# Two graph attention layers: the vectors W1 a1 and W1 a2 by dots on VectorE, a fourth tile of adj, weight work in single steps, constants made later

## The chip, the cores and the metric

The kernel runs on one core of a Trainium2 chip. Five engines work beside each other, each on its own list of instructions: TensorE (PE; its weight loads are counted as PEld), VectorE (DVE), ScalarE (ACT), GpSimd (POOL) and SyncE (SP), which only issues transfers. Transfers (DMAs) are issued by SP, ACT or POOL. The metric is the device time of one launch in microseconds (us); three runs of the kernel before gave 1781.02 us as their median.

## What is computed

```python
f = x @ Wf + bf;  g = x @ Wg + bg
e = jax.nn.relu(f @ g.T)                       # layer 0
attention = softmax(where(adj > 0, e, NEG), axis=1)
x = layernorm(x + attention @ (x @ W + bW))

h = x @ W1                                     # layer 1
e = leaky_relu(h @ a1 + (h @ a2).T, 0.2)
attention = softmax(where(adj > 0, e, NEG), axis=1)
x = layernorm(x + relu(attention @ h))
```

There are 2708 nodes with 1024 features; adj is 2708 x 2708 (int32), symmetric, with about 0.6% of its entries set. All is float32.

## The kernel before

**Algebra.** The score f g^T is x (Wf Wg^T) x^T with bias terms. So a prelude makes M = Wf Wg^T once, the bias rows c3 and rb, and for layer 1 the vectors u1 = W1 a1 and u2 = W1 a2, each repeated on all 128 partitions (`u1b`, `u2b`). Since adj is sparse, the prelude also turns each of its rows into a list of at most 40 neighbours; both layers then gather only these rows of x.

**Prelude, lists.** adj is cut into 22 blocks of 128 rows; the last has 20. For each block, `lists(b)` does: a load by SP into a tile of the pool `adjp` (three buffers), Relu to float on ACT with a row count (`tot`), a product with the falling ramp `iota` on POOL (line 409; block 0's in two cuts), 20 times the eight largest of 136 columns on VectorE (line 412), then the 40 largest of those 160 (five maxima at line 416 with a replacement between them at line 418), and counts (lines 420 and 424). `keep_lists(b - 3)` has ACT turn the list into indices and send it to memory (`LD`).

**Prelude, weights.** `weights()` is a generator whose steps are interleaved with the blocks, one step after each block from block 1 on. `turned` transposes a loaded 128-row tile of a weight matrix by eight TensorE transposes and two ACT copies; the tiles come through the pool `stage` (three buffers), loaded by ACT in the order Wg, Wf, W1. `m_product` is a sixteenth of M (eight products of 128x512), its ACT copy is kept in `late` and done at the next `flush()`. `c_product` makes the bias vectors of one half; its `take` ends with `row_parts`, which splits a row in three bfloat16 parts by casts, subtractions and small DMAs on POOL. bW goes through `row_parts` too. After c_product(0) stands a small product for the scalar `s0` (the ACT copy of tile `s`). Last come W1's eight transposed tiles and `u_product(0)` and `(1)`, whose `take` copies into `u1b` and `u2b`. These go on after the loop where the steps outlast the blocks.

**Order.** The engines' objects `pe`, `dve`, `act`, `pool` and `sp` are wrapped by `InOrder` (line 71 of the page is its helper): what they issue stays in program order on that engine. Instructions issued through `nc.gpsimd` and `nc.vector` are placed by a scheduler. Waits between engines follow from the tiles; a buffer of a pool is written again only when its last reader is done. At the head of POOL's list stand the constants (`ramp`, `stack`, `rep`, `early`, `lower`, `qcol`) and `iota`.

**After the lists.** Lines 454 to 501 rank the nodes by list length (VectorE with five small TensorE products) and write the orders `ids` and `idq`.

**Start of layer 0.** POOL gathers x of block 1 and 0 (`load_x`) and their lists (`load_lists`); VectorE makes `q_dot(1)` and `q_dot(0)`, then a minimum on the lists (`SL0`, in `first_gathers`) which releases the first gathers of neighbours into `ring`. TensorE makes the products with M of block 1 (`two_products`), ACT copies them four times over partitions (`Fr`), and VectorE's `dots` of unit 0 take them. Then follow `f_small` (block 0, in quarters summed by a second product), `x_turn(2)`, `f_product(2)`, the load of W into `Wt`, and a loop over the units: dots on VectorE, exp on ACT, sums over neighbours on TensorE (`po<-ring,st`), products with W (`pm<-Wt,xT`). The page's rows of some 700 matmuls are this loop in both layers. The end of this start reads:

```python
        q_dot(2)
        f_small()
        x_turn(2)
        load_x(3)
        load_lists(4)
        f_product(2)
        spread2 = q_spread(2)
        next(spread2)
        act.dma_start(Wt, W.rearrange("(k p) d -> p k d", p=P))
        dots(units[0], 0, len(units[0].tiles))
```

Of the kernel before, what the change touches and what calls it, by code (L numbers as in the profile page):

```python
# [106 lines left out]
def listed_path(ctx, tc, x, adj, Wf, bf, Wg, bg, W, bW, W1, a1, a2, out):  # L107
# [43 lines left out]
    nc.gpsimd.memset(ones3, 1.0)  # L151
# [4 lines left out]
    nc.gpsimd.memset(quad, 0.0)  # L156
    for q in range(Q):
        rows = slice(32 * q, 32 * q + 32)
        nc.gpsimd.tensor_copy(stack[rows], ident[rows, rows])
        nc.gpsimd.memset(quad[rows, q:q + 1], 1.0)  # L160
    for q in range(Q):
        nc.gpsimd.tensor_copy(rep[:, q, :], stack)
# [4 lines left out]
    nc.gpsimd.memset(ids[:, 0:1], 0)  # L167
# [4 lines left out]
    nc.gpsimd.memset(f1, 0.0)  # L172
# [4 lines left out]
    for t in scores:  # L177
        nc.gpsimd.memset(t, 0.0)
# [15 lines left out]
    with tc.tile_pool(name="pre", bufs=1) as pre:  # L194
        iota = pre.tile([P, N], F32, name="iota")
        nc.gpsimd.iota(iota, pattern=[[-1, N]], base=NONE, channel_multiplier=0,
# [3 lines left out]
        tot = pre.tile([P, NB], F32, name="tot")  # L200
        cnt = pre.tile([P, NB], F32, name="cnt")
# [7 lines left out]
        def ramp(name, count, step, base, dtype=F32, part=0):  # L209
            t = pre.tile([P, count], dtype, name=name)  # L210
            nc.gpsimd.iota(t, pattern=[[step, count]], base=base, channel_multiplier=part,
                           allow_small_or_imprecise_dtypes=True)
            return t

        fours = ramp("fours", QT, 4, 0)
        classes = ramp("classes", NCL, 1, 0)
        lows = ramp("lows", 32, 1, 0)
        highs = pre.tile([P, NG], F32, name="highs")
        rows512 = ramp("rows512", NB, 512, 0)
        part4 = ramp("part4", 1, 0, 0, part=4)  # L220
        lower = pre.tile([P, P], BF16, name="lower")
        nc.gpsimd.memset(lower, 1.0)
        nc.gpsimd.affine_select(lower, lower, pattern=[[1, P]], compare_op=ALU.is_gt, fill=0.0,
                                base=0, channel_multiplier=-1)
        early = pre.tile([P, NB, NB], F32, name="early")
        nc.gpsimd.memset(early, 1.0)
        nc.gpsimd.affine_select(early, early, pattern=[[1, NB], [-1, NB]], compare_op=ALU.is_gt, fill=0.0,
                                base=0, channel_multiplier=0)
        onesb = pre.tile([P, P], BF16, name="onesb")
        nc.gpsimd.memset(onesb, 1.0)  # L230
        qcol = pre.tile([P, 1], F32, name="qcol")
        for q in range(Q):
            nc.gpsimd.memset(qcol[32 * q:32 * q + 32], float(q))

        def fill_highs():
            nc.gpsimd.memset(highs[:, 0:1], float(GROUPS[0]))
            h = highs[:, 1:].rearrange("p (b k) -> p b k", k=4)
            at = 0
            for n, a, b in BLOCKS:
                for k, (g0, g1) in ((0, a), (2, b)):  # L240
                    if g1 == g0 + 1:
                        nc.gpsimd.iota(h[:, at:at + n, k:k + 2], pattern=[[2, n], [1, 2]], base=g0,
                                       channel_multiplier=0, allow_small_or_imprecise_dtypes=True)
                    else:
                        for i, g in enumerate((g0, g1)):
                            nc.gpsimd.memset(h[:, at:at + 1, k + i:k + i + 1], float(g))
                at += n

        with tc.tile_pool(name="adjp", bufs=3) as adjp, tc.tile_pool(name="cands", bufs=2) as cands, \
# [19 lines left out]
            order += [(W1, k) for k in range(KC)]  # L269
# [21 lines left out]

            def weights():


                late = []

                def flush():
                    while late:
                        late.pop(0)()
# [27 lines left out]
                def u_product(h, wT):  # L327

                    half = slice(h * 512, (h + 1) * 512)
                    pm = ps_m.tile([P, H, 512], F32, name="pm")  # L330
                    for i in range(KC):
                        for j in range(2):
                            pe.matmul(pm[64 * j:64 * j + 64, 0, :], ac[:, j, i:i + 1].to_broadcast([P, 64]),
                                      wT[:, i, :], start=(i == 0), stop=(i == KC - 1))

                    def take():
                        for j, u in enumerate((u1b, u2b)):
                            mine, other = 64 * j, 64 - 64 * j
                            act.copy(u[mine:mine + 64, half], pm[mine:mine + 64, 0, :])
                            for q in (0, 32):  # L340
                                act.copy(u[other + q:other + q + 32, half], pm[mine + q:mine + q + 32, 0, :])
                    late.append(take)


                four = pre.tile([32, P], F32, name="four")
                for i, v in enumerate((bg, bf, a1, a2)):
                    act.dma_start(four[8 * i:8 * i + 8], v.rearrange("(k p) -> k p" if i < 2 else "(k p) o -> k (p o)", p=P))
                cols = pre.tile([P, 4, KC], F32, name="cols")
                bgc, bfc, ac = cols[:, 0, :], cols[:, 1, :], cols[:, 2:4, :]
                WgT = {0: half_tile()}  # L350
                for k in range(4):
                    turned(WgT[0][:, :, k * P:(k + 1) * P])
                pt = ps_t.tile([P, 4, P], F32, name="pt")
                pe.transpose(pt[:, 0, :32], four, ident[:32, :32])
                act.copy(cols.rearrange("p v k -> p (v k)"), pt[:, 0, :32])
                yield
                WgT[1] = half_tile()
                for k in range(KC):
                    flush()
                    turned(WfT[:, :, k * P:(k + 1) * P])  # L360
                    if k >= 4:
                        turned(WgT[1][:, :, (k - 4) * P:(k - 3) * P])
                    m_product(k, 0)
                    if k in (2, 5):
                        half = slice(k // 3 * 512, k // 3 * 512 + 512)
                        brow = pre.tile([1, 512], F32, name="rest", bufs=3)
                        act.dma_start(brow, bW[half].rearrange("(o d) -> o d", o=1))
                        row_parts(brow, b3[:, half])
                    yield
                flush()  # L370
# [4 lines left out]
                nc.vector.scalar_tensor_tensor(t, bfc, 1.0, bgc, op0=ALU.mult, op1=ALU.mult, accum_out=t1)  # L375
                pt = ps_t.tile([P, 4, P], F32, name="pt")
                pe.matmul(pt[:, 0, 0:1], ones.to_broadcast([P, P]), t1, start=True, stop=True)
                act.copy(s0, pt[:, 0, 0:1])
                yield
                W1T = None  # L380
                for k in range(KC):
                    flush()
                    if k >= 4:
                        W1T = W1T or half_tile()
                        turned(W1T[:, :, (k - 4) * P:(k - 3) * P])
                    m_product(k, 1)
                    yield
                flush()
                c_product(1)
                yield  # L390
                flush()
                u_product(0, W1T)
                W1T = half_tile()
                for k in range(4):
                    turned(W1T[:, :, k * P:(k + 1) * P])
                yield
                flush()
                u_product(1, W1T)
                yield
                flush()  # L400

            def lists(b):
                n = nsize[b]
                t = adjp.tile([P, N], I32, name="adj")
                sp.dma_start(t[:n], adj[b * P:b * P + n, :])
                k = t.bitcast(F32)
                act.activation(k[:n], t[:n], AF.Relu, accum_out=tot[:n, b:b + 1])
                for cut in ([slice(0, 10 * SEG), slice(10 * SEG, N)] if b == 0 else [slice(0, N)]):
                    nc.gpsimd.tensor_tensor(k[:n, cut], k[:n, cut], iota[:n, cut], op=ALU.mult)  # L409
                cand = cands.tile([P, NSEG, 8], F32, name="cand")  # L410
                for s in range(NSEG):
                    nc.vector.max(cand[:n, s, :], k[:n, s * SEG:min((s + 1) * SEG, N)])  # L412
# [21 lines left out]
            steps = weights()  # L434
            for b in range(NB):
                lists(b)
                if b > 2:
                    keep_lists(b - 3)
                if b == 4:
                    fill_highs()  # L440

                if b > 0:
                    next(steps, None)
            for b in range(NB - 3, NB):
                keep_lists(b)
            for _ in steps:
                pass

        bc = lambda t, k, shape: t.unsqueeze(k).to_broadcast(shape)
        eq = pre.tile([P, NB, NCL], F32, name="eq")
        gt = pre.tile([P, NB, NCL], F32, name="gt")
# [1021 lines left out]
```

## Time and profile before

| what | time |
|---|---|
| median of three runs | 1781.02 us (1780.73 to 1785.28) |
| profiled execution | 1778.93 us |
| its span in the profile | 1777.1 us |
| end of the last list (VectorE) | 205.99 us |
| end of the ids | 217.92 us |
| first sums of unit 0 (TensorE) | 280.58 us |
| first product with W | 293.91 us |

The groups of instructions from 0 to 206 us with each shape by itself (line, engine, operation, tiles, shapes, count, then busy us, mean ns of one, and the idle time before them with what ended it):

```profile
L409 POOL TENSOR_TENSOR adj<-adj,iota 128x2708 f32<-128x2708 f32 x20 | 118.6, 5935 | 22.8 <-ACT adj L71 22.7
L412 DVE MAX8 cand<-adj 128x8 f32<-128x136 f32 x399 | 89.3, 286 | 37.2 <-POOL adj L409 37.2
L71 ACT ACTIVATE adj<-adj 128x2708 f32<-128x2708 int32 x21 | 51.8, 2465 | 25.6 <-DMA adj<-in_adj_dram 25.6
L416 DVE MAX8 L<-cand 128x8 f32<-128x160 f32 x105 | 33.8, 322 | 2.5
L418 DVE MATCH_REPLACE8 cand<-L,cand 128x160 f32<-128x160 f32 x84 | 25.9, 309 | 0.0
```

A mean of one can hold a wait inside a run of instructions: 20 maxima in a row take 4.11 us where nothing else of VectorE's stands between them. Idle time before a group is listed where it ends; it costs only if that engine is late for the end. Of an engine's idle time, the name behind the arrow is the instruction or transfer that came last.

### The profile page before, as it was taken

To read this page: it belongs to the slowest core of one execution; us is meant where nothing else is said; L and a number is where in the kernel's file an instruction comes from. 1 tells how busy PE (TensorE), PEld (TensorE's weight loads), DVE (VectorE), ACT (ScalarE), POOL (GpSimd) and SP (SyncE) were. 2 spreads that over 40 slices of the span, in tenths; PEclk is the share of its full clock that TensorE was granted. 3 is DMA by queue.
4 is the path that set the end of the run, shared out by engine and by line. 5 is a ranking of instruction groups with operands and counts; after the bars stand their busy time and mean duration, and the time that the engine had idled before them with its cause. 6 is when DMAs were issued, how large, how long until landed. Compare 5 with 4: busy or idle time off the path is not lost. (4 is left out here: it accounts for less than half of the span.)

```text
span 1777.1 us, 22911 instructions
## 1 busy us (share of the span) xinstructions
PE 1573.1 (89%) x7313; PEld 667.6 (38%) x7313; DVE 1171.4 (66%) x3539; ACT 636.4 (36%) x861; POOL 1182.5 (67%) x1191
## 2 busy tenths in 40 slices
PE   4999479899999999999999999637989988989996
PEld 2444234344444444444444444213333333333342
DVE  5879855888888888988888887513342433424442
ACT  4544454444444455555555544101111111111111
POOL 7878476467666666666666663177777777777740
PEclk9999779999999999999999999959989999999998
DMA  7646168568777777777777777299999999999960
GB/s 283 237 169 238 40 233 301 208 224 296 282 285 274 264 250 255 280 284 287 279 291 283 268 281 281 103 358 346 363 386 392 392 364 394 384 392 388 366 259 37
DMA packets 149982, 501.86 MB, mean 282 GB/s; under 512 B 32565, under 2 KB 32597, under 8 KB 147144
## 3 DMA queue, kind: packets, MB, share of 16 engines
q0 software_dynamic: 132032, 427.36, 64.8%
q1 hardware_dynamic: 10202, 55.72, 8.3%
q10 hardware_dynamic: 7618, 17.23, 2.7%
q8 instruction: 59, 0.97, 0.2%
q14 instruction: 71, 0.58, 0.1%
HBM read 509.64 MB, written 33.75 MB: 306 GB/s over the span
## 5 line engine op out<-in xcount | busy, mean ns | idle before, releaser
L71 POOL DMA_INDIRECT ring<-in_x_dram,SL x405 | 432.0, 1067 | 256.2 <-issue 89.0
L71 DVE SCALAR_TENSOR_TENSOR j<-ring,Fr 128x1024 bf16<-128x1024 f32 x402 | 494.9, 1231 | 77.0 <-DMA ring<-in_x_dram,SL 49.8
L71 ACT COPY Fr<-pm 32x1024 f32<-32x1024 f32 (+2 forms) x353 | 340.5, 965 | 20.0 <-PE pm L71 15.3
L71 PE MATMUL po<-ring,st 128*32 128x512 f32 x2660 | 338.6, 614 | 0.1
L71 POOL DMA_INDIRECT ring<-T,SL x260 | 259.6, 998 | 83.8 <-issue 58.0
L71 PE MATMUL pm<-M,xT 128*128 128x512 f32 (+1 forms) x704 | 309.7, 617 | 0.4 <-ACT xT L71 0.4
L71 PE MATMUL pm<-Wt,xT 128*128 128x512 f32 (+1 forms) x704 | 303.5, 599 | 0.0
L71 PE MATMUL pm<-M,yT 128*128 128x512 f32 (+1 forms) x704 | 298.5, 595 | 0.3 <-ACT yT L71 0.3
L71 ACT ACTIVATE scores<-scores 128x24 f32<-128x24 f32 (+5 forms) x44 | 9.8, 222 | 640.7 <-DVE scores L71 640.7
L71 PEld LDWEIGHTS pm<-M,yT 128*128 128x128 f32 (+1 forms) x704 | 127.2, 186 | 170.2 <-issue 169.7
L71 PEld LDWEIGHTS pm<-M,xT 128*128 128x128 f32 (+1 forms) x704 | 127.0, 190 | 170.6 <-issue 169.9
L71 PEld LDWEIGHTS pm<-Wt,xT 128*128 128x128 f32 (+1 forms) x704 | 125.0, 186 | 151.8 <-issue 151.4
L71 POOL DMA_INDIRECT more<-T,SL x145 | 144.1, 994 | 44.0 <-issue 32.8
L71 PEld LDWEIGHTS po<-ring,st 128*32 128x32 f32 x2660 | 102.5, 114 | 183.9 <-issue 180.0
L71 DVE TENSOR_SCALAR scores<-ring,f1q 128x2 f32<-128x2 f32 (+5 forms) x98 | 21.8, 245 | 211.3 <-DMA ring<-T,SL 209.6
L409 POOL TENSOR_TENSOR adj<-adj,iota 128x2708 f32<-128x2708 f32 (+3 forms) x23 | 130.5, 5684 | 24.9 <-ACT adj L71 24.8
L71 ACT ACTIVATE y<-po,ri 128x512 f32<-128x512 f32 (+1 forms) x88 | 55.8, 683 | 232.5 <-PE po L71 214.6
L412 DVE MAX8 cand<-adj 128x8 f32<-128x136 f32 (+2 forms) x440 | 97.2, 284 | 37.4 <-POOL adj L409 37.4
L71 PE MATMUL pm<-halfT,WfT 128*128 128x512 f32 x256 | 113.9, 600 | 1.1 <-ACT WfT L71 1.1
L71 POOL DMA_INDIRECT SL<-LD,idq x85 | 85.5, 1006 | 25.8 <-issue 20.9
L71 PE MATMUL pt<-rs,stack 128*32 128x1 f32 x680 | 14.1, 179 | 98.0 <-DVE rs L71 53.4
L71 PE MATMUL po<-more,st 128*32 128x512 f32 x580 | 94.2, 651 | 0.0
(198 smaller groups left out, 1416.9 us busy)
## 6 DMA issues: line engine op xcount, KB each, us to landing
adj<-in_adj_dram SPq DMA_DIRECT2D x21, 1354.0 KB, 5.8
X1S<-z SPq DMA_DIRECT2D x20, 512.0 KB, 6.4
ring<-in_x_dram,SL POOLq DMA_INDIRECT x405, 6.2
u1b<-X1S SPq DMA_DIRECT2D x11, 512.0 KB
rb<-X1S SPq DMA_DIRECT2D x10, 512.0 KB, 7.3
ring<-T,SL POOLq DMA_INDIRECT x260, 7.3
rows<-in_L_gnn_Wg_dram ACTq DMA_DIRECT2D x8, 512.0 KB, 4.5
rows<-in_L_gnn_Wf_dram ACTq DMA_DIRECT2D x8, 512.0 KB, 3.6
```

Source lines behind the costliest of these rows:

```text
L71: made = self.tc.keep_in_program_order(op(*args, **kwargs))
L409: nc.gpsimd.tensor_tensor(k[:n, cut], k[:n, cut], iota[:n, cut], op=ALU.mult)
L412: nc.vector.max(cand[:n, s, :], k[:n, s * SEG:min((s + 1) * SEG, N)])
```

## The change

1. W1 a1 and W1 a2: the eight tiles of W1 and the two u products leave the prelude. W1 is loaded whole by SP into `Wt`, which lies where the weights' pool lay; a1 and a2 are spread over the partitions by two POOL DMAs; 16 dots on VectorE (`u_dots`, 4 of them ahead of `q_dot(1)`, 12 between the two q spreads) make `ucols`, 16 TensorE products with the identity turn them (`u_spread`), four ACT copies write `u1b` and `u2b`. W is loaded into the same `Wt` later, as before, behind these.
2. `adjp` has four buffers. Block 0 is loaded and passed through Relu in two cuts, the products of blocks 0 and 1 are in two cuts; a small Relu before the first load brings ACT's table in.
3. The block of 20 rows lies on 4 x 32 partitions with 677 columns each (five maxima in place of 20, four POOL products, four POOL loads) and is taken as the twelfth of the 22.
4. The steps of `weights()` are single tiles (cost 1) and single products (cost 6); after block i they go on until their sum reaches 2i, from the third block on 6.5i - 13.5. bW is loaded once, ahead.
5. Constants are made behind the first products (at blocks 2 to 5, `highs` at 8), in POOL's program order.
6. Ranking: `same` is first on VectorE, its product with `early` is on POOL. Its tiles lie in a pool of their own.
7. Start of layer 0: block 2 is transposed before the small product, whose first part uses a tile of `ps_s`; `f_product(2)` stands ahead of the small product's second part. The copy `Fr[0, 0]` and the load of W stand after the first u copies.

```diff
-            order += [(W1, k) for k in range(KC)]
...
-        with tc.tile_pool(name="adjp", bufs=3) as adjp, tc.tile_pool(name="cands", bufs=2) as cands, \
+        with tc.tile_pool(name="adjp", bufs=4) as adjp, tc.tile_pool(name="cands", bufs=2) as cands, \
...
+                brow = u1b[0:1, :]
+                act.dma_start(brow, bW.rearrange("(o d) -> o d", o=1))
...
+                if b == NB - 1:
+                    k = tail.bitcast(F32)
+                    act.activation(k, tail, AF.Relu, accum_out=tails)
...
+                    for c in range(4):
+                        rows = slice(32 * c, 32 * c + 32)
+                        pool.tensor_tensor(k[rows], k[rows], iota[rows, c * quarter:(c + 1) * quarter],
+                                                op=ALU.mult)
+                    for s in range(NSEG // 4):
+                        nc.vector.max(cand4[:, s, :], k[:, s * SEG:min((s + 1) * SEG, quarter)])
...
+            act.activation(tot2, ones, AF.Relu)
+            for i, b in enumerate(blocks):
                 lists(b)
...
+                if 2 <= i < 6:
+                    next(some, None)
+                if i == 6:
+                    pool.memset(tail, 0)
+                    for c in range(4):
+                        pool.dma_start(tail[32 * c:32 * c + few, :], adj[N - few:, c * quarter:(c + 1) * quarter])
...
+                if i in (13, 15):
+                    u, a = (u1b, a1) if i == 13 else (u2b, a2)
+                    pool.dma_start(u, a.rearrange("d o -> (d o)").partition_broadcast(P))
+
+                flush()
+                while done < (2 * i if i < 3 else 6.5 * i - 13.5):
+                    cost = next(steps, None)
...
         Wt = new_pool("w0", 1).tile([P, KC, D], F32, name="Wt")
+
+        sp.dma_start(Wt, W1.rearrange("(k p) d -> p k d", p=P))
...
+        ucols = small.tile([P, 2, KC], F32, name="ucols", bufs=1)
+
+        def u_dots(k0, k1):
+            for k in range(k0, k1):
+                for i, u in enumerate((u1b, u2b)):
+                    dot(Wt[:, k, :], u, P, ucols[:, i, k:k + 1])
...
+        u_dots(0, 2)
         q_dot(1)
         q_dot(0)
...
+        for _ in spread1:
+            pass
+        u_dots(2, KC)
+        for _ in spread0:
+            pass
+        xTs[2] = tp.tile([P, KC, P], F32, name="xT")
+        turn2 = turn(xb[2], nrows[2], xTs[2])
+        next(turn2)
+
+
+        small_f = split_product(xTs.pop(0), M, yp.tile([P, D], F32, name="y"), 0,
+                                ps_s.tile([P, H, 512], F32, name="po"))
+        next(small_f)
...
+        next(small_f)
         q_dot(2)
-        f_small()
-        x_turn(2)
         load_x(3)
         load_lists(4)
+        spreads = [u_spread(0), u_spread(1)]
+        next(spreads[0])
         f_product(2)
+        for _ in spreads[0]:
+            pass
+        next(spreads[1])
+        Fr[0, 0] = zs[:, :D]
+        act.copy(Fr[0, 0], flat(whole(small_f)))
+        for _ in spreads[1]:
+            pass
         spread2 = q_spread(2)
         next(spread2)
         act.dma_start(Wt, W.rearrange("(k p) d -> p k d", p=P))
```

## The prediction

> **What bounds the kernel now.** I read the page first, then a table of stages, then waits and timeline of the first 300 us, where the edits lie. From the page:
>
> ```profile
> span 1777.1 us, 22911 instructions
> ...
> PE 1573.1 (89%) x7313; PEld 667.6 (38%) x7313; DVE 1171.4 (66%) x3539; ACT 636.4 (36%) x861; POOL 1182.5 (67%) x1191
> ...
> PE   4999479899999999999999999637989988989996
> PEld 2444234344444444444444444213333333333342
> DVE  5879855888888888988888887513342433424442
> ```
>
> A slice is 44.4 us. The prelude is the first five; from the seventh on TensorE is full. The table of stages (columns: window, length, busy time of each engine, granted clock, DMA share, GB/s) gives the contrast:
>
> ```profile
> 180.00:206.00 26.00, 14.41 (x78) 6.32 (x74) 24.61 (x126) 13.86 (x24) 16.92 (x10) 0.91 0.17 48
> 206.00:230.00 24.00, 8.98 (x48) 6.31 (x49) 12.91 (x36) 6.05 (x11) 8.11 (x8) 0.50 0.11 29
> 380.00:1150.00 770.00, 741.64 (x3260) 314.45 (x3256) 662.47 (x1496) 370.86 (x449) 486.69 (x460) 1.00 0.74 268
> ```
>
> In the steady stage TensorE works 741.64 of 770 us, and nothing there is edited: a microsecond won before it should reach the end, since nothing in it hangs on an absolute time. At the end of the prelude VectorE is the late engine (24.61 of 26), and TensorE's last product of W1 ends at 196.08, 11.4 us before its next work. The 23 us of TensorE work that the change removes are therefore no gain by themselves. What sets the end of the prelude is the chain load of adj, Relu (ACT), product with iota (POOL), maxima (VectorE), block after block. Its waits, from 0 to 206 us (total, times, longest):
>
> ```profile
> DVE cand L412 <- POOL adj L409: 37.4, 13, 12.8
> ...
> POOL adj L409 <- ACT adj L71: 24.8, 11, 7.2
> ...
> ACT s L71 <- PE pt L71: 6.7, 1, 6.7
> ...
> POOL part L256 <- DMA rest<-in_L_gnn_bW_dram: 5.5, 2, 3.5
> ```
>
> Of 206 us VectorE is busy 162.0; 37.4 of the 44 idle are these 13 waits. Where they and the next ones lie, by the timeline (start, length):
>
> ```profile
> 6.76 1.28 ACT L71 ACT_TABLE_LOAD   x1 [6.76 <-DMA adj<-in_adj_dram]
> ...
> 13.85 2.11 DVE L412 MAX8 cand<-adj 128x8 f32<-128x136 f32 x10 [12.77 <-POOL adj L409]
> ...
> 198.02 4.10 DVE L412 MAX8 cand<-adj 20x8 f32<-20x136 f32 x20 [0.28 <-POOL adj L409]
> ...
> 223.47 1.23 DVE L71 SCALAR_TENSOR_TENSOR j<-xb,rb 128x1024 bf16<-128x1024 f32 x1 [5.55 <-DMA xb<-in_x_dram,ids]
> ...
> 244.87 0.22 DVE L71 TENSOR_SCALAR q<-pt,s 128x4 f32<-128x4 f32 x1 [14.64 <-PE pt L71]
> ```
>
> The reader sees a late start, a block of only 20 rows that costs VectorE as much as a full one and comes last, and two holes (5.55 and 14.64) after it.
>
> **What the Trainium skill says.** "ScalarE: Activation LUTs", What ACT_TABLE_LOAD costs, gives about 1283 ns; the trace has 1.28 us, on the path. "DMA: Bandwidth & Descriptors", Latency and other measured facts, gives a transfer a fixed cost of about 2 us; no half load is in this trace to test it. The same page, Issuing engines are not separate DMA queues, says that transfers started by any engine share the 16 DMA engines and interleave: the 4096 KB of W, issued at 264.89 beside gathers, landed near 280.6, 15.7 us, and the DMA view has 412 to 423 GB/s over the stretch. "GPSIMD Engine Reference", Key points, says that GpSimd shares SBUF interfaces with VectorE for instructions of two SBUF inputs; the dots here take 1.21 to 1.23 us with POOL quiet and 1.25 to 1.29 beside gathers, so I price the new dots at 1.27.
>
> **The change, part by part**, on the profiled execution.
>
> *Start.* 1354 KB landed 5.95 us after issue (0.81 to 6.76). With 2 us fixed, half takes an estimated 4.0 and lands at 4.8. Half a Relu is 1.25 (2.46 for all), half a product 3.06 (the row of 128x1360), 0.3 for hand-overs: first maximum at 9.4 instead of 13.85, the table being loaded during the transfer. -4.4. Bounds -2 (halves land together at 6.8) to -5.5.
>
> *Block 1 in halves.* VectorE waited 3.79 at 22.74 for a whole product of 5.94. With half of it, about 1 is left: -2.8.
>
> *Tail of 20 rows.* At the end it takes 198.02 to 205.99, 8.0. In the new layout five maxima (some 1.3), four copies of 0.2 and the same selection (202.16 to 205.99, 3.8) are 5.9: -2.1. Its four products on 677 columns are 5.93/4 each, so POOL gains nothing. Its place in the middle only moves it.
>
> *bW once, early.* POOL's cast waited 3.5 for bW at 53, and the product queued behind made VectorE wait 3.60 at 62.02: -3.5. The second wait (2.0 at 80) hit nothing.
>
> *ACT held behind TensorE.* The copy of s waited 6.74 for TensorE's c product, with the Relu of the next block behind it; POOL then waited 7.22 and VectorE 2.91, 5.40 and 1.69, 10.0 in all. Smaller weight steps and a fourth adj buffer let a Relu through earlier, but the in-order queue and TensorE's pace stay: 6.5 units a block at 145/124 = 1.17 us (the windows up to 206 sum to 168 us of TensorE work; less 8 transposed tiles at 1.15 and two products at 7.03, 23) is 7.6 us a block, as long as VectorE's. I take two thirds, -6.5; bounds 0 and -10.
>
> *Onto POOL.* The constants (5 us between 4.08 and 8.2 plus qcol, hidden behind the first load before) and six DMA issues (four for the tail, two broadcasts; an indirect one takes 1.0) now stand between products: 10 us more in a queue whose mults and row parts take 154. POOL idled about 33 us between 10.76 and 198, so most is absorbed: +2.5, bounds 0 and +10.
>
> End of lists: -4.4 - 2.8 - 2.1 - 3.5 - 6.5 + 2.5 = -16.8, at about 189 instead of 206. The rank work after it, 11.9 us, stays: one product of 0.64 moves to POOL under other work, -0.3.
>
> *W1.* Its load waits for TensorE's last c product. That is paced into the last block's turn, and I place its end at 172 to 182 (TensorE from about 12, 145 busy, 15 to 25 idle; before it idled 12 from 15.9 to 196). With 12 to 15.7 us for 4096 KB it lands at 184 to 198. ids end at about 201, so it's in time. Four dots (5.1) fit into the hole of 5.55, twelve (15.2) into that of 14.64: +0.6. Behind them on VectorE stand q_dot and the minimum that releases the first ring gathers; this is the cover to watch. TensorE gets 16 transposing matmuls of some 0.13 (eight transposes take 1.04), 2 us, in its hole of 9.19 or after.
>
> *Start of layer 0.* f_product of block 2 begins near 255 instead of 264.8 (it needn't wait for the small product's repetition). But the sums of unit 0, at 280.58 before, need exp on ACT, which now stands behind the y copy and four u copies and the z copy (9 x 0.6 = 5 us more): I get 277.5, -2.6. Against it, W is issued behind those copies, near 275.8 instead of 264.9, and lands near 291.5 to 298; its first product is due at 291. TensorE waits 0 to 7; I take 2.6, so this part is 0 (bounds -4 and +5).
>
> Sum: -16.8 - 0.3 + 0.6 + 0 = -16.5. The span 1777.1 becomes 1760.6; the profiled run was 1778.93 and becomes 1762.4. The median of the runs, 1781.02, stands 2.1 above the profiled run: 1764.5, said as 1764.
>
> **Rivals.**
> A. The lists are bound by POOL or by ACT behind TensorE after all: the 6.5 isn't won, the 10 us on POOL cost 5. Then -4.4 - 2.8 - 2.1 - 3.5 + 5 + 0.3 = -7.5: 1773. For it: TensorE's 7.6 and VectorE's 7.5 us a block; POOL's 24.8 us of waits for Relu. Against it: those waits are tied to single places.
> B. Also the start of layer 0 is won, W landing before it is due (at 412 GB/s 4096 KB are 10 us, an end at 286): -16.5 - 4 = 1760; with the whole 10 of the ACT wait 1757. Against it: gathers share the engines.
> C. W1 lands late. The place is VectorE's first four dots: every microsecond after ids + 0.4 delays q_dot, the minimum, each ring gather and all that follows, one for one. It decides from a landing at 201.4; the gain is gone at 218 and at 225 the kernel takes 1788. For that TensorE's last c product must end near 210, which takes over 50 us of idle time in the prelude. If W lands late too (7 instead of 2.6), 206 is enough. For it: TensorE is now paced, not run ahead, and ACT's queue couples it to the blocks. Against it: it idled 12 us before.
> D. The gain is swallowed by a slack before the steady stage. The gathers and TensorE start from ids, and TensorE is full from 380; I see no slack of 10 us. About 1781.
>
> **How the numbers follow.** The forecast has 0.50, A 0.17, B 0.14, C 0.11, D 0.08. 0.3% is 5.3 us, about what a measurement tells from no change: 1775.7 to 1786.4. Faster: the forecast, B and most of A, 0.79. Same: D and a part of A and C, 0.10. Slower: C, 0.11. The likeliest case's own range is 1757 to 1770; holding 8 in 10 with A and B it is 1753 to 1777.
>
> **What would show it.** Right: first maximum at 9 to 10; last selection of a list at 186 to 192; no W1 transposes; W1 landed before ids; no hole over 1 us around the first dots; sums of unit 0 some 17 to 20 us earlier, the same length from there to the end. Wrong: VectorE idle by more than 16 us on adj after its first maximum (A); a wait of VectorE for W1 (C); TensorE waiting over 5 us for W (start of layer 0).

## The result, and the profile after

The changed kernel takes 1781.76 us, the kernel before 1782.62 (medians of 20 runs each); the ratio is 0.9994, with a 95% interval of 0.9982 to 1.0006. No change can be measured, where 1764 was forecast. The profiled execution has a span of 1779.0 us and took 1781.02. For two of the experiments below, e8 and e9, every kernel was about 13% slower on their chip (the kernel before: 2014.87 us) and the profiled executions were slow ones, so of these two only the ratio and the prelude are used; e9's prelude agrees with that of the same kernel on another chip (e9b).

From the page of the changed kernel:

```profile
span 1779.0 us, 22751 instructions
...
PE 1560.0 (88%) x7217; PEld 666.1 (37%) x7217; DVE 1198.2 (67%) x3559; ACT 624.1 (35%) x840; POOL 1195.6 (67%) x1210
...
PE   4799298899999999999999999727989898999996
...
DVE  4899985888988888888888887612433434424442
```

TensorE has 13 us less to do and VectorE 27 us more. VectorE's first slice fell from 5 to 4, although its first maximum is 4.3 us earlier: there is new idle time near the start. The marks of the prelude, each the start or end of an instruction in the two traces:

| us | before | after | difference |
|---|---|---|---|
| first maximum | 13.85 | 9.58 | -4.3 |
| end of the last list | 205.98 | 202.31 | -3.7 |
| end of the ids | 217.92 | 216.69 | -1.2 |
| q dot of block 1 (x landed) | 223.47 | 223.13 | -0.3 |
| first dot of unit 0 | 246.92 | 246.92 | 0 |
| first sums of unit 0 | 280.58 | 278.85 | -1.7 |
| first product with W | 293.91 | 294.10 | +0.2 |

So the start was won, the lists added nothing to it where another 12.4 us had been forecast, the ranking behind them gave 2.4 us back, and the last of the gain was gone at 247 us. The first sums still came 1.7 us earlier but took 1.7 us longer (8.77 for 7.07), and at the first product with W both kernels stand within 0.2 us. A difference of 1.9 us in the spans lies inside the scatter of the runs (1778.0 to 1789.64).

VectorE's and POOL's waits from 0 to 206 us in the changed kernel (total, times, longest):

```profile
DVE cand L423 <- POOL adj L71: 16.2, 6, 8.5
DVE cand L423 <- POOL quad L71: 13.3, 1, 13.3
...
POOL part L265 <- DMA u1b<-in_L_gnn_bW_dram: 5.1, 1, 5.1
POOL adj L71 <- ACT adj L71: 5.0, 4, 2.6
```

POOL waits for ACT only 5.0 us where it waited 24.8: the expected relief came. But VectorE has a new wait of 13.3 in one piece (`quad` is a constant that POOL fills right behind the product of block 2). The timeline of VectorE, then that of POOL (start, length, and in brackets the idle time before):

```profile
9.58 2.11 DVE L423 MAX8 cand<-adj 128x8 f32<-128x136 f32 x10 [8.51 <-POOL adj L71]
...
39.67 4.11 DVE L423 MAX8 cand<-adj 128x8 f32<-128x136 f32 x20 [13.30 <-POOL quad L71]
53.05 4.11 DVE L423 MAX8 cand<-adj 128x8 f32<-128x136 f32 x20 [5.22 <-POOL adj L71]
...
116.77 7.96 DVE L402 COPY cand<-cand 20x40 f32<-20x40 f32 x4
```

```profile
24.00 0.60 POOL L265 CAST part<-u1b 1x512 bf16<-1x512 f32 x1 [5.12 <-DMA u1b<-in_L_gnn_bW_dram]
...
32.29 0.60 POOL L265 CAST part<-rest 1x512 bf16<-1x512 f32 x1 [2.79 <-DMA rows<-part]
...
33.73 5.92 POOL L71 TENSOR_TENSOR adj<-adj,iota 128x2708 f32<-128x2708 f32 x1
...
39.77 0.60 POOL L265 CAST part<-u1b 1x512 bf16<-1x512 f32 x1
...
47.11 5.91 POOL L71 TENSOR_TENSOR adj<-adj,iota 128x2708 f32<-128x2708 f32 x1
```

The reader sees that the casts of `row_parts` on bW (line 265) stand on POOL before the product of block 2 (33.73) and before that of block 3 (47.11). In the program they belong to much later weight steps. They go through `nc.gpsimd`, so that only their data binds them; with bW loaded at the start nothing holds them back, and the scheduler put them there. Block 2's Relu was done at 23.98; its product began 9.75 us later, behind a first set of parts that itself stood still for 2.79 us until one of its small transfers had landed.

### The profile page after: what moved, and what is told of

It reads as the page before. It is cut to its first block, busy times and chain, and to the rows that moved or that the text cites. A ratio compares the mean times of both kernels' runs of the same rounds, so it can differ in the third digit from the quotient of the medians.

```text
span 1779.0 us, 22751 instructions
## 1 busy us (share of the span) xinstructions
PE 1560.0 (88%) x7217; PEld 666.1 (37%) x7217; DVE 1198.2 (67%) x3559; ACT 624.1 (35%) x840; POOL 1195.6 (67%) x1210
## 5 line engine op out<-in xcount | busy, mean ns | idle before, releaser
L71 POOL DMA_INDIRECT ring<-in_x_dram,SL x405 | 436.6, 1078 | 257.5 <-issue 88.7
L71 PE MATMUL pm<-M,xT 128*128 128x512 f32 x672 | 306.1, 609 | 0.0
L71 PEld LDWEIGHTS pm<-M,xT 128*128 128x128 f32 x672 | 126.6, 193 | 162.2 <-issue 162.2
L71 POOL TENSOR_TENSOR adj<-adj,iota 128x2708 f32<-128x2708 f32 (+2 forms) x23 | 124.5, 5427 | 8.9 <-ACT adj L71 5.0
L423 DVE MAX8 cand<-adj 128x8 f32<-128x136 f32 (+1 forms) x420 | 93.3, 284 | 29.5 <-POOL adj L71 16.2
```

What stands on the lines that cost most here:

```text
L71: made = self.tc.keep_in_program_order(op(*args, **kwargs))
```

## The experiments

All of them start from the changed kernel. Times are in us; the ratios are to the kernel before, measured beside it on the same chip. "Parts" are the casts, subtractions and small transfers of `row_parts`.

| kernel | last list | ids | first sums | first W product | ratio (95%) |
|---|---|---|---|---|---|
| changed | 202.31 | 216.69 | 278.85 | 294.10 | 0.9994 (0.9982 to 1.0006) |
| e1: bW's parts behind blocks 8, 10 | 199.81 | 214.20 | 276.45 | 291.48 | 0.9991 (0.9976 to 1.0007) |
| e2: c parts before the last list copies | 201.74 | 214.66 | 276.54 | 291.56 | 0.9992 (0.9976 to 1.0008) |
| e3: e1 and e2 | 199.46 | 212.39 | 275.09 | 291.00 | 0.9986 (0.9975 to 0.9997) |
| e4: e3, exp and W first | 200.12 | 213.06 | 273.12 | 286.45 | 0.9970 (0.9954 to 0.9986) |
| e5: tail copies on ACT | 200.55 | 214.93 | 275.95 | 291.29 | 0.9969 (0.9956 to 0.9982) |
| e6: e4 and e5 | 196.55 | 209.47 | 269.91 | 283.24 | 0.9945 (0.9926 to 0.9964) |
| e7: e6, bW's parts behind the last product | 184.91 | 208.41 | 268.70 | 282.03 | 0.9938 (0.9922 to 0.9955) |
| e8: e7, parts behind blocks 16, 18 | 194.43 | 207.35 | - | - | 0.9920 (0.9862 to 0.9978) |
| e9: changed, bW's and c parts behind the last product | 188.83 | 209.13 | - | - | 0.9945 (0.9901 to 0.9989) |
| e9b: the kernel of e9 again | 188.83 | 209.04 | 270.21 | 285.24 | 0.9960 (0.9944 to 0.9975) |
| e10: e7, same times early on VectorE | 185.70 | 201.95 | 263.08 | 276.41 | 0.9923 (0.9895 to 0.9952) |

**e1, bW's row parts later.**

```diff
-                    if k in (2, 5):
-                        row_parts(brow[:, half], b3[:, half])
...
+                if i in (8, 10):
+                    row_parts(u1b[0:1, half], b3[:, half], pool)
```

> The changed kernel with bW's two sets of row parts taken out of the weight steps and issued in POOL's program order behind the products of blocks 8 and 10. Theory 1 (in the changed kernel the row parts of bW stand on POOL ahead of the products of blocks 2 and 3; VectorE's waits of 13.30 and 5.22 us come from that): these two waits shrink to about 4 in all, the last list ends at 186 to 191 us instead of 202.3, and the time falls by 11 to 15 us, to about 1768. Theory 2 (the Relu of blocks 2 and 3 is late anyway, behind weight copies that wait for their transfers, and row parts only fill the gap): the waits stay above 12, the last list ends after 197, time within 5 us of the changed kernel's. Theory 3 (whatever the lists gain is lost between ids and the first sums): last list at 186 to 191, but first sums of unit 0 after 275 and time within 5 us of 1782.

Neither theory as it stood. From VectorE's timeline of e1:

```profile
30.20 4.11 DVE L420 MAX8 cand<-adj 128x8 f32<-128x136 f32 x20 [3.97 <-POOL quad L71]
...
90.14 0.30 DVE L420 MAX8 cand<-adj 128x8 f32<-128x136 f32 x1 [6.18 <-POOL adj L71]
108.89 1.10 DVE L396 MAX8 cand<-tail 128x8 f32<-128x136 f32 x5 [1.83 <-POOL tail L71]
110.03 12.21 DVE L399 COPY cand<-cand 20x40 f32<-20x40 f32 x4
```

The two early waits fell from 18.52 to 3.97, so their cause is shown; POOL's product of block 2 now begins at 24.25, right behind its Relu (done at 24.08), so that the 3.97 that are left come from the Relu. But the list end moved by 2.5 only: at 90 us VectorE waits 6.18 again, behind the parts at their new place, and the four copies of the tail grew from 7.96 to 12.21. What had been lost early was now lost later. That points to POOL being late as a whole, and to the copies.

Narrow windows of the same traces take the four copies apart (start and length in us):

| copy | e1 | changed | e9b (below) |
|---|---|---|---|
| 1 | 110.03, 0.17 | 116.77, 1.60 | 102.14, 2.72 |
| 2 | 110.21, 5.97 | 118.38, 5.87 | 104.87, 5.87 |
| 3 | 116.20, 5.85 | 124.27, 0.17 | 110.76, 0.17 |
| 4 | 122.06, 0.18 | 124.46, 0.27 | 110.94, 0.31 |
| POOL's two products | 110.23 to 122.01 | 112.38 to 124.22 | 98.86 to 110.71 |

A copy outside POOL's products takes 0.17 to 0.31 us. One that meets a product ends within 0.05 us of that product's end, and the next copy then meets the second product.

**e2, the last c product's parts earlier.**

```diff
+            for _ in steps:
+                pass
+            flush()
             for b in blocks[-3:]:
                 keep_lists(b)
-            for _ in steps:
-                pass
-            flush()
```

and these parts and the product of `same` with `early` in POOL's program order.

> The changed kernel with the copies and row parts of the last c product ahead of the last three list copies on ACT, and on POOL ahead of the product of same with early, so that they run while VectorE still makes lists. Theory 1b (POOL's work beside the ranking slows VectorE's instructions with two inputs): from the end of the last list to the last ids 11.9 us as in the kernel before, instead of 14.4; ids 2.4 us earlier; time 1 to 3 us less. Rival (the slower ranking comes from the new order of its instructions): it stays at 14.4.

From the end of the lists to the ids it is 12.9 us, where the changed kernel had 14.4 and the kernel before 11.9. In the changed kernel the ranking's instructions ran beside POOL's work. VectorE, then POOL:

```profile
203.40 1.42 DVE L488 TENSOR_TENSOR gt<-cls,classes 128x242 f32<-128x242 f32 x1
...
207.35 0.62 DVE L504 TENSOR_SCALAR hl<-ranki 128x22 int32<-128x22 int32 x1
...
209.11 2.08 DVE L516 TENSOR_TENSOR hot<-hlf,highs 128x935 bf16<-128x935 f32 x1
```

```profile
203.29 1.25 POOL L484 TENSOR_TENSOR same<-same,early 128x484 f32<-128x484 f32 x1 [19.92 <-DVE same L483]
204.49 0.78 POOL L265 CAST part<-rest 1x512 bf16<-1x512 f32 x1
...
207.33 0.60 POOL L265 CAST part<-rest 1x512 bf16<-1x512 f32 x1
...
208.76 1.44 POOL L269 TENSOR_TENSOR rest<-rest,part 1x512 f32<-1x512 f32 x1
210.26 1.39 POOL L265 CAST part<-rest 1x512 bf16<-1x512 f32 x1
```

In the kernel before, with POOL idle, the same three took:

```profile
206.44 0.39 DVE L455 TENSOR_TENSOR gt<-cls,classes 128x242 f32<-128x242 f32 x1
...
210.38 0.18 DVE L474 TENSOR_SCALAR hl<-ranki 128x22 int32<-128x22 int32 x1
...
211.70 1.13 DVE L486 TENSOR_TENSOR hot<-hlf,highs 128x935 bf16<-128x935 f32 x1
```

The first overlaps `same` with `early`, the second a cast, the third a subtraction and a cast; POOL's side is longer too in places (a cast takes 0.60, a subtraction 1.15 alone). In e2 the parts are gone from there, and the product of `same` still runs beside `gt`:

```profile
202.83 1.41 DVE L488 TENSOR_TENSOR gt<-cls,classes 128x242 f32<-128x242 f32 x1
...
207.13 0.18 DVE L504 TENSOR_SCALAR hl<-ranki 128x22 int32<-128x22 int32 x1
...
208.45 1.13 DVE L516 TENSOR_TENSOR hot<-hlf,highs 128x935 bf16<-128x935 f32 x1
```

So the parts cost 1.5 us, and the 1.0 us that is left to the kernel before is `gt`, 1.41 for 0.39, beside the product that the change itself moved to POOL. The theory holds, and the rival (the new order of the ranking's instructions) has next to nothing left to explain.

**e3, both.**

> Both edits together. If they add: last list at 186 to 191 us, ids 12 us later, first sums of unit 0 at 261 to 266 us instead of 278.85, time 1764 to 1769. If the start of layer 0 absorbs: first sums after 272.

The lists didn't come to the forecast, so it doesn't test the start of layer 0 as meant. The 2.9 us that the first product with W is earlier are found in the time (0.9986, 2.5 us).

**e4, exp and the load of W first on ACT.**

```diff
+        act.dma_start(Wt, W.rearrange("(k p) d -> p k d", p=P))
+        dots(units[0], 0, len(units[0].tiles))
...
+        soft(units[0])
         Fr[0, 0] = zs[:, :D]
         act.copy(Fr[0, 0], flat(whole(small_f)))
...
-        act.dma_start(Wt, W.rearrange("(k p) d -> p k d", p=P))
-        dots(units[0], 0, len(units[0].tiles))
...
-        soft(units[0])
```

> Both edits, and on ACT the load of W and the exp of unit 0 ahead of the copies of z, u2b. In the changed kernel exp stood 6.7 us behind them, and TensorE waited 1.6 and 1.2 us before the sums and then ran them at a clock of 0.79. If that wait counts: first sums 2 to 4 us earlier than with both edits alone, time 2 to 5 us less. If TensorE's order (f product, u turns, small product, sums) is the limit: less than 1 us.

In the changed kernel, ACT and then TensorE (the last column of a line is the idle time before it):

```profile
275.13 1.01 ACT L71 COPY z<-pm 128x1024 f32<-128x1024 f32 x1 [13.35 <-PE pm L71]
275.24 0.39 ACTq L71 DMA_DIRECT2D Wt<-in_L_gnn_W_dram  x1
276.04 1.08 ACT L71 COPY u2b<-pt 128x512 f32<-128x512 f32 x2
276.99 0.24 ACT L71 ACTIVATE scores<-scores 128x16 f32<-128x16 f32 x1
```

```profile
278.85 8.77 PE L71 MATMUL po<-ring,st 128*32 128x512 f32 x60 [0.33 <-issue]
...
294.10 7.13 PE L71 MATMUL pm<-Wt,xT 128*128 128x512 f32 x16
```

ACT idles 13.35 us until the small product, with exp queued behind. In e4 exp ran at 265.54, in e3 at 273.36; the sums began at 273.12, 2.0 us earlier than in e3, and took 7.07 us, as in the kernel before, for 9.65 in e3; the first product with W came 4.55 us earlier than in e3. The wait counted. The sums' 8.77 us go with a granted clock of 0.79 from 280 to 288 us (1.00 in the kernel before), after two holes of 1.59 and 1.15 in TensorE's work.

**e5, the tail's copies on ACT.**

```diff
-                        nc.vector.tensor_copy(cand[:n, c * NSEG // 4:(c + 1) * NSEG // 4, :], cand4[rows])
+                        act.copy(cand[:n, c * NSEG // 4:(c + 1) * NSEG // 4, :], cand4[rows])
```

with the copies and the selection after them issued two blocks later.

> The changed kernel with one edit: the four copies of the tail's candidates to the first 20 partitions run on ACT, two blocks later, in place of VectorE. In the changed kernel they are shown as 7.96 us on VectorE, and in the first experiment as 12.21, each time ending within 0.6 us of the end of POOL's two products beside them. Theory 4 (a VectorE copy of that form stands still while POOL's product runs): the copies take 0.2 to 0.4 us each on ACT, the tail's turn on VectorE falls from 13 us to about 6, the last list ends at 194 to 196 us instead of 202.3, and the time falls by 5 to 8 us. Rival 4b (a copy between partition groups is slow in itself): over 1 us each on ACT too. Rival 4c (POOL or ACT is late next): last list ends after 200 and VectorE shows new waits.

```profile
117.34 0.93 ACT L71 COPY candt<-cand 20x40 f32<-20x40 f32 x4
```

All four take 0.93 us on ACT: rival 4b falls. In their place VectorE waits for POOL, 2.85, 1.78, 1.31 and 1.99 between 120 and 147 us, 7.9 in all. The last list is only 1.8 us earlier, so rival 4c holds here: the copies had been standing in front of a wait. The first product with W is 2.6 us earlier than in the kernel before, which would be a ratio of 0.9985; the measured 0.9969 (0.9956 to 0.9982) is lower, and no run here shows why.

**e6, with e4.**

> The kernel of e4 with the same edit. If the costs found so far add: last list at 188 to 190 us, first sums of unit 0 at 261 to 264, first product with W at 275 to 278, time 10 to 12 us under e4's, 1763 to 1766. If the parts of bW, behind blocks 8 and 10, are late next on POOL: last list after 194, a wait of VectorE for POOL of over 6 us near 90 us.

Between the two cases: the last list at 196.55 (e4: 200.12), the wait near 90 us is 5.60, and further waits for POOL of 2.07, 6.18, 1.77, 1.26 and 2.05 lie between 108 and 143 us. POOL is the late engine there.

**e7, bW's parts behind the last product.**

```diff
-                if i in (8, 10):
-                    row_parts(u1b[0:1, half], b3[:, half], pool)
...
             flush()
+            for half in (slice(0, 512), slice(512, 1024)):
+                brow = pre.tile([1, 512], F32, name="rest", bufs=3)
+                act.dma_start(brow, bW[half].rearrange("(o d) -> o d", o=1))
+                row_parts(brow, b3[:, half], pool)
             for b in blocks[-3:]:
```

> The kernel of e6 with bW loaded and its row parts made after the last product, where POOL is idle, in place of behind blocks 8 and 10. Expected: the wait of 6.2 us near 90 us goes, last list 4 to 6 us earlier than in e6, time 3 to 6 us less. If these parts then run beside the ranking: ranking over 13 us and no gain.

The last list ends at 184.91, 11.6 us earlier than in e6 (4 to 6 were expected). This is what the prediction gave for the changed kernel (189), and more. But the ids end at 208.41, 23.5 us later, the second case of the expectation. POOL, then VectorE:

```profile
172.31 0.60 POOL L71 CAST part<-rest 1x512 bf16<-1x512 f32 x1 [5.12 <-ACT rest L71]
...
195.63 1.22 POOL L71 TENSOR_TENSOR same<-same,early 128x484 f32<-128x484 f32 x1
```

```profile
196.88 0.66 DVE L511 TENSOR_REDUCE rank<-same 128x22 f32<-128x484 f32 x1 [6.34 <-POOL same L71]
197.45 1.22 DVE L71 SCALAR_TENSOR_TENSOR j<-Wt,u2b 128x1024 bf16<-128x1024 f32 x1
```

The parts of c and bW keep POOL until 195.6, and the ranking's product waits behind them. Behind this wait, three of the first four dots of W1 (1.22 us each) also stand between the ranking's instructions, ahead of the ids.

**e8, the parts behind blocks 16 and 18.**

```diff
+                if i in (16, 18):
+                    row_parts(brow, b3[:, half], pool)
```

> The kernel of e7 with bW's row parts behind the products of blocks 16 and 18 in place of behind the last, so that POOL is free for the ranking. In e7 the last list ended at 184.91 us but the ids only at 208.41: POOL worked on row parts until 196, and VectorE waited 6.34 us for POOL's product of same with early, which stood behind them. If that is the whole loss: last list at 185 to 188 us, ids 12 to 14 us later (197 to 202), first product with W at 270 to 275, time 7 to 11 us under e7's, 1760 to 1764. If the start of layer 0 can't follow: first product with W after 279 and time within 3 us of e7's.

A miss: the last list is at 194.43, where 185 to 188 was expected. VectorE's timeline:

```profile
151.87 0.30 DVE L418 MAX8 cand<-adj 128x8 f32<-128x136 f32 x1 [4.00 <-POOL adj L71]
170.93 0.30 DVE L418 MAX8 cand<-adj 128x8 f32<-128x136 f32 x1 [3.99 <-POOL adj L71]
```

Each set of parts keeps POOL for 6.9 us between two products (139.04 to 145.90 for the first; 5.6 of them busy) and costs VectorE 4 us even here. An estimate from these traces: a block takes VectorE 7 to 8 us and POOL's product 5.93, so that POOL has 1 to 2 us a block to spare, far less than 6.9.

**e9 and e9b, the changed kernel with the parts behind the last product** (e2's edit and that of e7, no other).

> The changed kernel with the row parts of bW and of the last c product behind the last product on POOL, ahead of the product of same with early; the tail's copies stay on VectorE and the start of layer 0 stays as in the changed kernel. It tells what the tail's copies cost once POOL isn't late: if VectorE stands still in them as long as POOL's two products run (10 to 12 us), the last list ends at 191 to 195 us against 184.91 with the copies on ACT (e7), and no list wait lies between 104 and 131 us. If the copies only fill a wait for POOL, as e5 suggests: 185 to 188 us.

> The kernel of e9 once more. From its first trace the last list is expected at 189 us, ids at 209, first product with W at 282 to 286 (the start of layer 0 is that of the changed kernel, exp behind the copies), time 0.994 to 0.997 of the kernel before. A first product with W after 291, or a time within 0.2% of the kernel before, would mean that the start of layer 0 takes back what the lists gain.

The last list is at 188.83 in both runs, 13.5 us earlier than in the changed kernel. Against e2 (201.74), from which e9b differs only in the load and the parts of bW, it is 12.9. The ids are at 209.04 and the first product with W at 285.24, as expected from e9; the ratio is 0.9960. In e9b, VectorE and POOL:

```profile
102.14 9.11 DVE L397 COPY cand<-cand 20x40 f32<-20x40 f32 x4
```

```profile
98.86 11.85 POOL L71 TENSOR_TENSOR adj<-adj,iota 128x2708 f32<-128x2708 f32 x2 [3.26 <-ACT adj L71]
```

The copies end at 111.25 and the two products at 110.71. They cost about 3.9 us here (188.83 against 184.91 with the copies on ACT), between the two cases of the expectation: VectorE does stand still beside the products, but in e7 it waits for POOL at the same place four times, 7.7 us in all, and these waits are gone here.

**e10, the ranking without POOL.**

```diff
-            pool.tensor_tensor(same, same, early, op=ALU.mult)
+            nc.vector.tensor_tensor(same, same, early, op=ALU.mult)
```

> The kernel of e7 with the product of same with early on VectorE, as in the kernel before, so that no step of the ranking waits for POOL, whose row parts of bW run beside it. If the wait for POOL was the loss: last list at 185 us, ids at 197 to 200, first product with W at 271 to 275, time 6 to 10 us under e7's (in e7 0.9938 of the kernel before; here 0.988 to 0.990). If POOL's work beside it slows the ranking as much as the wait did: ids after 204.

The ids end at 201.95, 6.5 us earlier than in e7, later than the 197 to 200 expected: the ranking runs beside POOL's parts (the product of `same` takes 1.60 us, 0.64 in the kernel before), and one of the dots of u1 and one of u2 were placed ahead of the ids. The first product with W is at 276.41 (271 to 275 expected), 17.5 us before that of the kernel before, and the ratio is 0.9923 (0.9895 to 0.9952; 0.988 to 0.990 expected), 1766.54 us in six runs against 1782.24. This version is faster than the kernel before and, going by the ratios, than the changed kernel.

## Why the prediction was wrong, point by point

| step | forecast, us | measured in the changed kernel |
|---|---|---|
| start | -4.4 | -4.3, first maximum at 9.58 for 9.4 |
| block 1 in halves | -2.8 | -2.9, the wait went from 3.79 to 0.88 |
| tail of 20 rows | -2.1 | +5.0, its turn took 13.0 us (115.63 to 128.6) where it had taken 8.0 |
| bW early, ACT held, POOL's additions | -3.5, -6.5, +2.5 | -0.8: old waits of 19.99 us gone, new ones of 19.20 |
| ranking | -0.3 | +2.4 |
| dots of W1 | +0.6 | they fit: holes of 5.55 and 14.64 became 1.36 and 0.55 |
| start of layer 0 | 0 | +1.4 between ids and the first product with W |

The first four rows sum to -3.0, and the list end moved by -3.7; the rest stays open. The forecast for these rows was -16.8. The steps that failed are three, all of them work on POOL or beside it. The prediction's own sign of this, VectorE idle by more than 16 us on adj after its first maximum, came: 21.0 us (16.2 and 13.3, less the 8.5 ahead of it).

*bW once, early* was priced as a gain of 3.5 us. The step looked at the wait for bW's transfer and not at what else had tied `row_parts` to its place: that transfer itself. Without it the parts of bW moved in front of the products of blocks 2 and 3, with waits of VectorE of 13.30 and 5.22 us. e1 shows the cause, and e9b against e2 the price: behind the last product they leave the lists 12.9 us earlier.

*Onto POOL* took the 33 idle microseconds of POOL as room and put 2.5 on 10 added. e1, e6 and e8 show that parts put at blocks 8, 16 and 18 come back as waits of 4 to 6 us. POOL's idle time in the kernel before lay in single waits for ACT, most of which the change removed (24.8 us became 5.0). What is left to spare is small in each block, and a set of parts in one place overruns it. Rival A had a late POOL, with 5 us for its price; the sum of rival A ended at 1773.

*Four copies of 0.2* were 7.96 us. The 0.2 is right for a copy that meets no product (0.17 in e1); a copy of VectorE that meets one stands still until the product ends, in all three traces taken apart above, while on ACT, beside the same products, the four take 0.93 us. The Trainium skill's "GPSIMD Engine Reference", Key points, says that GpSimd shares SBUF interfaces with VectorE and names contention with VectorE's 2-port modes and with two SBUF inputs. Only the second was used in the prediction, and only for the dots. These copies have one input, which leaves the first of the two; which mode they ran in no trace here shows, so this reason stays an argument. While POOL is late anyway, they cost little by themselves (1.8 us in e5).

Of the ranking the prediction said that it stays and that the product on POOL wins 0.3. POOL was idle beside it before; after the change the parts of the last c product, whose ACT copies stand behind the last list copies, run there, and so does that product. e2 won back 1.5 of the 2.4 us; the other 1.0 is the price of the product on POOL.

The last 1.2 us between ids and 247 us went in two places. x of block 1 took longer to land (0.3 us of gain left at the q dot); and the first product with M took 9.40 us in place of 9.03, so that both kernels finished it at 237.0. The granted clock was 0.50 up to about 232 us in both. The Trainium skill's "TensorE: Matmul & The Clock Gate", What's actually happening, says that the clock is released by a window of about 3.4 us that runs free and does not start with the kernel. The traces agree: over all thirteen, the clock rose between 3.0 and 6.0 us after this product had begun, and the product took 8.63 to 10.11 us. So the gain that was lost at this product looks like chance, not like a cost of the change.

The start of layer 0 was to win 2.6 us up to the first sums and lose as much to a wait for W. (The prediction's 277.5 against 280.58 would be 3.1, not 2.6.) Counted from the ids, the first sums came only 0.5 us earlier: exp was priced as standing behind some more copies, 5 us, but one of these, the copy of z, itself stood still for 13.35 us until the small product was done. And the wait for W was 0.4 us at most, where 2.6 had been taken: from the first sums to the first product with W it took 1.9 us longer, 1.7 of them in the sums at the clock of 0.79. In e4, with exp ahead of these copies, it is 60.1 us from the ids to the first sums, for 62.7 in the kernel before, which is the gain that was forecast, and the sums take 7.07.

What held: the start, with its mechanism: the Relu of the first half of block 0 began at 4.91 us, for an estimated landing at 4.8, and ACT's table was loaded during the transfer. W1 was loaded in time (TensorE's last c product ended at 185.5, a little later than the 172 to 182 given; the transfer was issued at 185.56, took 12.7 us and landed by 198.3, the ids came at 216.7), so rival C never came near. With the parts out of the way the lists of e9b end at 188.83, close to the 189 of the forecast; that is partly luck, since the tail of 20 rows still costs 3.9 us there. And most of a gain at the start reaches the end (against rival D): over e4, e6, e7, e9b and e10 the first product with W is earlier by 7.5, 10.7, 11.9, 8.7 and 17.5 us, and the time is lower by 5.3, 9.8, 11.0, 7.1 and 13.7 (by the ratio and the median of the kernel before beside it), 71 to 93% of it.

## What to carry to other kernels

A load that is moved ahead frees whatever had waited for it; look where a scheduler puts these instructions, on every engine, before counting the wait as won. Idle time of an in-order engine is room only where no one waits for what is queued behind; with the waits that made it gone, the engine may be the bound, and small work between two of its large instructions costs a good part of its length (4.0 of 6.9 us in e8). When work is put beside another engine, look in a trace for instructions of the same shape with and without the neighbour's work beside them.

## What the runs showed of the hardware

Four VectorE copies of 20x40 float32 took 7.96, 12.21 and 9.11 us beside POOL's products of 128x2708, and 0.93 us on ACT; a single one took 0.17 us outside a product and up to 5.97 within one, and each that met a product ended within 0.05 us of the product's end. The maxima didn't slow beside these products: 20 in a row take 4.11 us, and those of the tail in the kernel before, with POOL idle, 4.10. Of VectorE's instructions with two inputs, 128x242 took 1.42 for 0.39 us beside POOL's product of 128x484; 128x935 took 2.08 for 1.13 and 128x484 took 1.60 for 0.64 us beside POOL's casts and subtractions. An instruction with one input slowed too: the shift of 128x22 integers took 0.62 for 0.18 us beside a cast.
